# Down products two columns behind, up's last sum kept in PSUM, and the last additions shared: a feed-forward stage at the end of a two-layer kernel

## The chip, the core and the metric

The kernel runs on one core of a Trainium2 chip. The core has a matrix engine (TensorE, PE in the profile), a vector engine (VectorE, DVE), a scalar engine (ScalarE, ACT), a general engine (GpSimd, POOL) and a queue that issues transfers (SyncE, SP). PE multiplies a loaded 128x128 weight block with up to 512 columns and writes into PSUM, a small memory of eight banks; one bank holds 512 numbers for each of 128 partitions. DVE and ACT read and write PSUM and SBUF, the large on-chip memory; POOL works here on SBUF alone. The metric is the device time of one execution in microseconds (us). Three runs of the kernel before took 881.0, 881.89 and 882.64 us, median 881.89.

## What is computed

Two layers, each an attention and a feed-forward part with residual sums, over 8 sequences of 128 tokens of width 512. The change touches only the last part, a gated feed-forward network with integer weights and a scale for each group of 128 inputs:

```python
def dequantize(imatrix, scales, zeros, group_size, out_dtype):
    rs = jnp.repeat(scales, group_size, axis=0)
    rz = jnp.repeat(zeros, group_size, axis=0)
    return ((imatrix.astype(rs.dtype) - rz.astype(rs.dtype)) * rs).astype(out_dtype)

gate = jax.nn.silu(jnp.dot(x, gate_proj))     # (1024, 512) x (512, 1792)
up = jnp.dot(x, up_proj)
return jnp.dot(gate * up, down_proj)          # (1024, 1792) x (1792, 512)
```

Its input is the layer norm of x, and its result is added to x.

## The kernel before

Everything ahead of this part (about 714 of 881 us) is the same in both kernels. The feed-forward part works transposed: the hidden dimension of 1792 is cut into 14 columns of 128 (`NI = 14`), and the tokens into two halves of 512 (`hf`). The layer-normed input stands as a high and a low part (`xn2`), the weights as exact small integers, so a product of 512 tokens takes two matmuls, one for the low and one for the high part (L858, L859).

A *unit* (`unit`, L852) is one group of 128 inputs for one column and both halves: four matmuls into a PSUM tile of two banks (`f`; `ps_f` has four of them, which is all of PSUM), and then the scaling by the group's scale while the tile is emptied. The first unit of a sum is copied out by ACT (L863). A later one is added to the sum in SBUF either by DVE in one instruction (`scalar_tensor_tensor`, L869) or, for `eng == "A"`, by ACT, which copies it scaled into a tile `tmp` (L866, two buffers), and POOL, which adds `tmp` to the sum (L867).

For a column c there are four units for gate and four for up. Their sums are built in pairs: units 0 and 1 into one tile, 2 and 3 into another (L881: `a = g - g % 2`), and POOL adds the two tiles (`merge`, L892 to L894; letters `gm` and `um`). In the last column the four go into one tile, with no merge. Then ACT takes the silu (`S`, L900), DVE multiplies with up (`gated`, `H`, L904), ACT rounds the product to its high part `h_h` (`cast`, `C`, L911), and POOL subtracts to get the low part `h_l` (`rest`, `L`, L918; DVE does it for the last column). Four down units multiply h with the down weights and add into `acc`, 128 x 4 x 2 x 512 numbers in SBUF.

`ORDER` gives the order of the columns. Columns 0, 1 and 2 have had their first token half done earlier, among the last rounds of attention; what is left of them is half a column (units of two matmuls). They stand at the second, the fourth and the last place of `ORDER`. In the last four columns of the loop, `a0` to `a3` add the first-half down units of the last column.

The loop over the first 13 columns (L964 to L968) emits each column by a string of letters, in which `d` is a down unit of the column that `DOWN` names, `LAG = 3` columns earlier:

```python
emit(f"g0 d0 g2 g1 u0 g3 gm d1 u2 {a}u1 d3 d2 u3 um S" + (" H C L" if i < NI - 2 else ""), i)
```

A scheduler lays out the loop's instructions on their engines; each engine then works through its own list in order and waits where an input or a buffer isn't there. In PE's list every column of the loop reads, in units, g d g g u g d u u d d u from the column on that has down units. The tail (from L970) is laid out in the order in which it is written: the last column's gate and up units, between them the 12 down units of the three columns before it (`downs`, with a letter for the engine, V for DVE and A for ACT with POOL), its product, cast and rest, its four half down units, and the end: PE turns `acc` back in 32 transposes (L1009), DVE adds it to x in eight additions of 128x512 (L1011), and SP sends each one out (L1012).

Apart from the value of `LAG` (L118) the diff starts at L838; the functions that it touches and the loop are printed here.

Of the kernel before, what the change touches and what calls it, by code (L numbers as in the profile page):

```python
# [9 lines left out]
F32 = mybir.dt.float32  # L10
# [3 lines left out]
ALU = mybir.AluOpType  # L14
# [3 lines left out]
P = 128  # L18
D = 512
KT = D // P  # L20
NB = 8
HB = 4
TOK = HB * P
# [6 lines left out]
NI = IC // P  # L30
# [4 lines left out]
def f32(ap):  # L35
    return ap.bitcast(F32)
# [3 lines left out]
def tile_layers(ctx: ExitStack, tc: tile.TileContext, t, out: bass.AP):  # L40
    nc = tc.nc

    def pool(stack, name, bufs, space=None, side="left"):
        kw = {"side": side}
        if space is not None:
            kw["space"] = space
        return stack.enter_context(tc.tile_pool(name=name, bufs=bufs, reuse_waits="tile", **kw))
# [7 lines left out]
    ident = const.tile([P, P], F32, name="ident")  # L55
# [58 lines left out]
    xs = [const.tile([P, HB, D], F32, name=f"xs{hf}") for hf in range(2)]  # L114


    NE = 3
    LAG = 3  # L118
    skv = ctx.enter_context(ExitStack())
    cpool = pool(skv, "cpool", 1, side="right")  # L120
    kvp = pool(skv, "kvp", 2, side="right")
# [195 lines left out]
    A, B = layer0(0), layer0(1)  # L317
# [363 lines left out]
    for i in range(3 * NI):  # L681
        m, c = ("gate", "up", "down")[i % 3], i // 3
# [36 lines left out]
    xn2, xnb, xst = {}, {}, {}  # L719
# [118 lines left out]

    fw = pool(ctx, "fw", 3)
    fa = pool(ctx, "fa", 1)  # L840
    fh = pool(ctx, "fh", LAG)
    fp = pool(ctx, "fp", 2, side="right")
    ps_f = pool(ctx, "ps_f", 4, PSUM)

    acc = fa.tile([P, KT, 2, TOK], F32, name="acc")

    def weights(m, c):
        wf = fw.tile([P, D], F32R, name=f"wf_{m}")
        nc.sync.dma_start(f32(wf), wint[m, c])
        return wf  # L850

    def unit(eng, wf, g, rhs, s, dst, first, hs=(0, 1)):  # L852

        ps = ps_f.tile([P, 2, TOK], F32, name="f")
        w = wf[:, g * P : (g + 1) * P]
        for hf in hs:
            rh, rl = rhs(hf)
            nc.tensor.matmul(ps[:, hf, :], w, rl, start=True, stop=False)  # L858
            nc.tensor.matmul(ps[:, hf, :], w, rh, start=False, stop=True)  # L859
        sl = slice(hs[0], hs[-1] + 1)  # L860
        ps, dst = ps[:, sl, :], dst[:, sl, :]
        if first:
            nc.scalar.activation(dst, ps, AF.Copy, scale=s)  # L863
        elif eng == "A":
            a2 = fa.tile([P, 2, TOK], F32, name="tmp", bufs=2)[:, sl, :]
            nc.scalar.activation(a2, ps, AF.Copy, scale=s)  # L866
            nc.gpsimd.tensor_tensor(dst, dst, a2, ALU.add)  # L867
        else:
            nc.vector.scalar_tensor_tensor(dst, ps, s, dst, ALU.mult, ALU.add)  # L869

    def late(c):
        return nc.vector if c == ORDER[-1] else nc.gpsimd

    hts, wfs, gu, ths = {}, {}, {}, {}

    def up_unit(m, g, c):
        s_sb = sg_sb if m == "gate" else su_sb
        if g == 0:
            wfs[m] = weights(m, c)

        a = 0 if c == ORDER[-1] else g - g % 2  # L881
        if g == a:
            gu[m, g] = fp.tile([P, 2, TOK], F32, name=f"{m}{g}", bufs=2)
        unit(
            "V", wfs[m], g, lambda hf: (xn2[hf][0][:, g, :], xn2[hf][1][:, g, :]),
            s_sb[:, c, g : g + 1], gu[m, a], g == a, (1,) if c < NE else (0, 1),
        )

    def part(ap, c):
        return ap[:, 1:, :] if c < NE else ap  # L890

    def merge(m, c):  # L892
        a, b = (part(gu[m, g], c) for g in (0, 2))
        late(c).tensor_tensor(a, a, b, ALU.add)  # L894

    def silu(c):
        ga = part(gu["gate", 0], c)
        ths[c] = fh.tile([P, 2, TOK], F32, name="th", bufs=3)
        th = part(ths[c], c)
        nc.scalar.activation(th, ga, AF.Silu)  # L900

    def gated(c):
        th = hts[c] = ths.pop(c)
        nc.vector.tensor_tensor(part(th, c), part(th, c), part(gu["up", 0], c), ALU.mult)  # L904

    def cast(c):
        th = hts[c]
        hh, hl = (fh.tile([P, 2, TOK], F32R, name=f"h_{p}") for p in "hl")
        if c < NE and c != ORDER[-1]:
            nc.scalar.copy(hh[:, 0, :], early[c])  # L910
        nc.scalar.copy(part(hh, c), part(th, c))  # L911
        hts[c] = (th, hh, hl)

    def rest(c):
        th, hh, hl = hts[c]
        if c < NE and c != ORDER[-1]:
            late(c).tensor_tensor(hl[:, 0, :], early[c], f32(hh[:, 0, :]), ALU.subtract)
        late(c).tensor_tensor(part(hl, c), part(th, c), part(f32(hh), c), ALU.subtract)  # L918
# [5 lines left out]
    def down_unit(o, c, hs=None, eng=None):  # L924
        if o == 0 and hs != (1,):
            wfs["down", c] = weights("down", c)
        hh, hl = first_h if hs == (0,) else hts[c][1:]
        if eng is None:
            eng = "A" if o in on_act(c) else "V"
        unit(  # L930
            eng, wfs["down", c], o, lambda hf: (hh[:, hf, :], hl[:, hf, :]),
            sd_sb[:, o, c : c + 1], acc[:, o], c == ORDER[0], hs or (0, 1),
        )
# [4 lines left out]
    def first_half():  # L938
        c = ORDER[-1]
        first_h.extend(fh.tile([P, 1, TOK], F32R, name=f"h1_{p}", bufs=1) for p in "hl")  # L940
        nc.scalar.copy(first_h[0][:, 0, :], early[c])
        nc.gpsimd.tensor_tensor(first_h[1][:, 0, :], early[c], f32(first_h[0][:, 0, :]), ALU.subtract)


    ORDER = [c for i in range(NE - 1) for c in (NE + i, i + 1)] + list(range(2 * NE - 1, NI)) + [0]

    DOWN = {i: (i - LAG,) for i in range(LAG, NI + LAG)}

    def emit(seq, i):
        c = ORDER[i] if i < NI else NI  # L950
        for it in seq.split():
            k, j = it[0], it[1:]
            if k in "gu" and c < NI:
                m = "gate" if k == "g" else "up"
                merge(m, c) if j == "m" else up_unit(m, int(j), c)
            elif k == "a":
                down_unit(int(j), ORDER[-1], (0,))
            elif k == "d":
                for p in DOWN.get(i, ()):
                    down_unit(int(j), ORDER[p])  # L960
            elif k in "SHCL" and c < NI:
                {"S": silu, "H": gated, "C": cast, "L": rest}[k](c)

    for i in range(NI - 1):  # L964
        if i == NI - 6:
            first_half()
        a = f"a{i - NI + 5} " if i >= NI - 5 else ""
        emit(f"g0 d0 g2 g1 u0 g3 gm d1 u2 {a}u1 d3 d2 u3 um S" + (" H C L" if i < NI - 2 else ""), i)  # L968
    ET = mybir.EngineType
    with tc.manual_schedule(engines={ET.PE, ET.DVE, ET.Activation, ET.Pool}):  # L970

        c = ORDER[-1]
        p = iter([(o, ORDER[i]) for i in range(NI - 1 - LAG, NI - 1) for o in range(KT)])

        def downs(engs):
            for e in engs:
                down_unit(*next(p), eng=e)

        up_unit("gate", 0, c)
        up_unit("gate", 1, c)  # L980
        downs("A")
        up_unit("gate", 2, c)
        up_unit("gate", 3, c)
        gated(ORDER[-2])
        downs("A")
        up_unit("up", 0, c)
        silu(c)
        cast(ORDER[-2])
        rest(ORDER[-2])
        up_unit("up", 1, c)  # L990
        downs("V")
        up_unit("up", 2, c)
        up_unit("up", 3, c)
        downs("V")
        gated(c)
        cast(c)
        downs("AV")
        rest(c)
        downs("VAVVAV")
        for o, e in zip(range(KT), "VAVV"):  # L1000
            down_unit(o, c, (1,), e)
        for hf in range(2):
            xt = xs[hf]
            for b in range(0, HB, 2):
                tp = ps_f.tile([P, 2, TOK], F32, name="f")
                for i in range(2):
                    cols = slice((b + i) * P, (b + i + 1) * P)
                    for o in range(KT):
                        nc.tensor.transpose(tp[:, i, o * P : (o + 1) * P], acc[:, o, hf, cols], ident)  # L1009
                for i in range(2):  # L1010
                    nc.vector.tensor_tensor(xt[:, b + i, :], tp[:, i, :], xt[:, b + i, :], ALU.add)  # L1011
                    nc.sync.dma_start(out[hf * HB + b + i], xt[:, b + i, :])  # L1012


# [49 lines left out]
```

## Time and profile before

| | |
|---|---|
| runs | 881.0, 881.89, 882.64 us |
| profiled execution | 882.38 us |
| its span, first to last instruction | 880.6 us |
| feed-forward part, first to last instruction | 713.9 to 880.6 us |
| first matmul of the last column's gate | 845.21 us |
| end of the last addition to x | 876.43 us |

The page of the profile gives, for the whole span, the busy time of each engine and the chain of work that ended last. The timeline lists instructions in order of time: start, duration, engine, line, operation, output and inputs with their shapes, and in brackets how long the engine stood idle before it and what ended that. The waits sum up who waited for whom. The busy time by stretches gives for each piece of time the busy us of PE, PEld, DVE, ACT and POOL with the numbers of instructions, the clock that PE was granted (1.00 is full), the share of the DMA engines and GB/s. An engine that is behind its inputs shows no idle time; one that waits shows whom it waited for, and the last of several inputs is the one named.

### The profile page before, as it was taken

The numbers are of one execution on the slowest core, as the hardware profiler recorded it, in microseconds if no ns is written. First come the engines' busy times: TensorE is split into PE (matmuls) and PEld (weight loads), VectorE is DVE, ScalarE is ACT, GpSimd is POOL, SyncE is SP. The second block draws the span as 40 slices with busy tenths as digits, with TensorE's granted clock in tenths as the row PEclk, the third lists the DMA queues.
The fourth block names the chain that finished last, engine by engine and source line by source line (L and its number), as shares of the span: only waits on it lengthen the run. The fifth ranks groups of instructions, "written<-read, shape, count | busy, mean of one in ns | idle before, by whom it ended". The sixth has DMA issues, their size and how long they took to land.

```text
span 880.6 us, 14074 instructions
## 1 busy us (share of the span) xinstructions
PE 852.4 (97%) x4568; PEld 716.8 (81%) x4568; DVE 627.1 (71%) x1049; ACT 438.7 (50%) x1565; POOL 518.2 (59%) x571
## 2 busy tenths in 40 slices
PE   6999999999999999999999999999999989999985
PEld 5889998899788888888888888888878767788764
DVE  6513697775777777777777777666786887889887
ACT  5323444244544455544555444444555568666652
POOL 4551684234665555555555555765454568899884
PEclk9899999999999999999999999999999999999998
DMA  8522342524777778777777786544234412222102
GB/s 298 137 96 97 133 137 91 144 97 168 251 246 236 212 249 250 241 210 248 241 231 221 252 250 217 178 145 143 94 129 138 132 36 73 72 73 72 48 25 96
DMA packets 115833, 141.01 MB, mean 160 GB/s; under 512 B 14128, under 2 KB 59952, under 8 KB 115760
## 3 DMA queue, kind: packets, MB, share of 16 engines
q1 hardware_dynamic: 115760, 140.12, 50.6%
q8 instruction: 36, 0.59, 0.3%
q14 instruction: 37, 0.30, 0.1%
HBM read 97.62 MB, written 42.47 MB: 159 GB/s over the span
## 4 chain that ended last, share of the span: by engine, by line
PE 83%; POOL 6%; DVE 6%; ACT 2%; issue 2%; DMA 1%; SPq 0%; DVEq 0%; POOLq 0%; ACTq 0%
PE mm L74 9%; PE mm L76 9%; PE mm L75 9%; PE f L858 6%; PE o L76 6%; PE o L74 6%; PE o L75 6%; PE f L859 6%; PE s L540 6%; PE tr L567 3%; PE kv L76 3%; PE kv L75 3%; PE kv L74 3%; PE o L581 2%; PE o L579 2%
## 5 line engine op out<-in xcount | busy, mean ns | idle before, releaser
L562 POOL TENSOR_TENSOR pr<-pr,rs 128x512 f32<-128x512 f32 x64 | 66.6, 1040 | 176.5 <-DVE rs L560 173.6
L601 DVE TENSOR_TENSOR xs<-o,xs 128x512 f32<-128x512 f32 x64 | 44.2, 691 | 95.4 <-PE o L76 95.4
L74 PE MATMUL mm<-wq_l,xnT_h 128*128 128x512 f32 x256 | 105.4, 412 | 0.0
L76 PE MATMUL o<-wo_h,aT_l 128*128 128x512 f32 x256 | 100.0, 390 | 0.7 <-DVE aT_l L589 0.7
L74 PE MATMUL o<-wo_l,aT_h 128*128 128x512 f32 x256 | 100.1, 391 | 0.2 <-DVE wo_l L66 0.2
L76 PE MATMUL mm<-wq_h,xnT_l 128*128 128x512 f32 x256 | 100.2, 392 | 0.0
L75 PE MATMUL mm<-wq_h,xnT_h 128*128 128x512 f32 x256 | 100.0, 391 | 0.0
L75 PE MATMUL o<-wo_h,aT_h 128*128 128x512 f32 x256 | 99.7, 389 | 0.0
L571 ACT CAST pT_h<-tr 128x512 fp32r<-128x512 f32 x64 | 37.5, 585 | 121.2 <-PE tr L567 121.2
L554 ACT ACTIVATE pr<-s,nm 128x128 f32<-128x128 f32 x256 | 90.8, 373 | 3.3 <-DVE nm L548 3.0
L588 ACT CAST aT_h<-o 128x512 fp32r<-128x512 f32 x64 | 37.6, 587 | 103.8 <-PE o L581 103.8
L74 PE MATMUL kv<-wkv_l,cT_h 128*128 128x256 f32 x256 | 73.6, 288 | 0.0
L507 ACT ACTIVATE junkq<-mm 128x128 f32<-128x128 f32 x256 | 67.3, 279 | 12.5 <-PE mm L76 6.1
L76 PE MATMUL kv<-wkv_h,cT_l 128*128 128x256 f32 x256 | 73.3, 286 | 0.0
L75 PE MATMUL kv<-wkv_h,cT_h 128*128 128x256 f32 x256 | 72.9, 285 | 0.0
L348 POOL TENSOR_TENSOR rrq<-msq,nhalf 128x4 f32<-128x4 f32 x64 | 64.7, 1011 | 5.3
L540 PE MATMUL s<-kT,qT 128*128 128x128 f32 x512 | 67.6, 275 | 0.0
L540 PEld LDWEIGHTS s<-kT,qT 128*128 128x128 f32 x512 | 62.3, 192 | 0.1
L572 DVE TENSOR_TENSOR pT_l<-tr,pT_h 128x512 fp32r<-128x512 f32 x64 | 44.0, 688 | 22.7 <-ACT pT_h L571 22.7
L76 PEld LDWEIGHTS o<-wo_h,aT_l 128*128 128x128 f32 x256 | 48.1, 188 | 11.5 <-DVE aT_l L589 1.5
L76 PEld LDWEIGHTS mm<-wq_h,xnT_l 128*128 128x128 f32 x256 | 48.1, 188 | 10.7
L74 PEld LDWEIGHTS o<-wo_l,aT_h 128*128 128x128 f32 x256 | 48.1, 188 | 10.7 <-DVE wo_l L66 0.6
(234 smaller groups left out, 2448.8 us busy)
## 6 DMA issues: line engine op xcount, KB each, us to landing
q_d<-qb SPq DMA_DIRECT2D x64, 256.0 KB, 2.0
qT<-q_d SPq DMA_DIRECT2D x64, 256.0 KB, 4.1
wst<-in_qpT SPq DMA_DIRECT2D x36, 256.0 KB, 4.6
wst<-in_opT SPq DMA_DIRECT2D x36, 256.0 KB, 3.8
wkv<-in_kvT SPq DMA_DIRECT2D x8, 512.0 KB, 4.5
v_d<-vh SPq DMA_DIRECT2D x16, 256.0 KB, 2.0
v_d<-vl SPq DMA_DIRECT2D x16, 256.0 KB, 2.3
kT_d<-kT SPq DMA_DIRECT2D x16, 256.0 KB, 2.7
```

The lines of the kernel that those rows point to most:

```text
L74: nc.tensor.matmul(o, ah, bl, start=start, stop=False)
L75: nc.tensor.matmul(o, ah, bh, start=False, stop=False)
L76: nc.tensor.matmul(o, al, bh, start=False, stop=stop)
L348: nc.gpsimd.tensor_tensor(r[:, :n], ms[:, :n], nhalf[:, :n], ALU.pow)
L507: nc.scalar.activation(junk, qps[u][:, r * HD : (r + 1) * HD], AF.Square, accum_out=ssq[:, r : r + 1])
L540: nc.tensor.matmul(sp[:, r, :], qTs[u][:, r, :], kTt[blocks[j]][:, :, i, :], start=True, stop=True)
L554: nc.scalar.activation(pr[:, r, :], sps[u][:, r, :], AF.Exp, bias=nms[u][:, r : r + 1], accum_out=sm[:, r : r + 1])
L562: nc.gpsimd.tensor_tensor(pr, pr, rs.unsqueeze(2).to_broadcast([P, NQ, P]), ALU.mult)
L572: nc.vector.tensor_tensor(pl, tps[u], f32(ph), ALU.subtract)
L601: nc.vector.tensor_tensor(x, pos[u], x, ALU.add)
L858: nc.tensor.matmul(ps[:, hf, :], w, rl, start=True, stop=False)
L859: nc.tensor.matmul(ps[:, hf, :], w, rh, start=False, stop=True)
```

## The change

`LAG` goes from 3 to 2, so each column's down units stand two columns behind its gate and up units, and the tail has eight full down units in place of 12. The pool of h tiles keeps its three buffers. For the column before the last, up's four units are summed in one tile without a merge, and in this and the last column the fourth sum is written into its own PSUM tile (`eng == "P"`), from which the product reads it. The tail is written in a new order with other engine letters; `tmp` has four buffers. At the end three of the eight additions to x go to ACT (a copy out of PSUM) and POOL (the addition).

```diff
-    LAG = 3
+    LAG = 2
...
-    fh = pool(ctx, "fh", LAG)
+    fh = pool(ctx, "fh", 3)
...
+        elif eng == "P":
+            nc.vector.scalar_tensor_tensor(ps, ps, s, dst, ALU.mult, ALU.add)
+            return ps
         elif eng == "A":
-            a2 = fa.tile([P, 2, TOK], F32, name="tmp", bufs=2)[:, sl, :]
+            a2 = fa.tile([P, 2, TOK], F32, name="tmp", bufs=4)[:, sl, :]
...
-        a = 0 if c == ORDER[-1] else g - g % 2
+        one = c == ORDER[-1] or (m, c) == ("up", ORDER[-2])
+        a = 0 if one else g - g % 2
...
-        unit(
-            "V", wfs[m], g, lambda hf: (xn2[hf][0][:, g, :], xn2[hf][1][:, g, :]),
+        upf[c] = unit(
+            "P" if one and (m, g) == ("up", KT - 1) else "V", wfs[m], g, lambda hf: (xn2[hf][0][:, g, :], xn2[hf][1][:, g, :]),
...
-        nc.vector.tensor_tensor(part(th, c), part(th, c), part(gu["up", 0], c), ALU.mult)
+        up = upf.pop(c)
+        nc.vector.tensor_tensor(part(th, c), part(th, c), part(gu["up", 0], c) if up is None else up, ALU.mult)
...
-        emit(f"g0 d0 g2 g1 u0 g3 gm d1 u2 {a}u1 d3 d2 u3 um S" + (" H C L" if i < NI - 2 else ""), i)
+        if i < NI - 2:
+            emit(f"g0 d0 g2 g1 u0 g3 gm d1 u2 {a}u1 d3 d2 u3 um S H C L", i)
+        else:
+            emit(f"g0 d0 g2 g1 u0 g3 gm d1 u1 {a}u2 d3 d2 u3 S", i)
...
+        gated(ORDER[-2])
         up_unit("gate", 0, c)
         up_unit("gate", 1, c)
+        cast(ORDER[-2])
         downs("A")
+        rest(ORDER[-2])
         up_unit("gate", 2, c)
         up_unit("gate", 3, c)
-        gated(ORDER[-2])
-        downs("A")
+        downs("V")
         up_unit("up", 0, c)
         silu(c)
-        cast(ORDER[-2])
-        rest(ORDER[-2])
         up_unit("up", 1, c)
-        downs("V")
+        downs("VA")
         up_unit("up", 2, c)
         up_unit("up", 3, c)
+        gated(c)
+        downs("A")
+        cast(c)
         downs("V")
-        gated(c)
-        cast(c)
+        rest(c)
         downs("AV")
-        rest(c)
-        downs("VAVVAV")
+
+        def turn(hf, b, engs):
+            xt = xs[hf]
+            tp = ps_f.tile([P, 2, TOK], F32, name="f")
+            for i in range(2):
+                cols = slice((b + i) * P, (b + i + 1) * P)
+                for o in range(KT):
+                    nc.tensor.transpose(tp[:, i, o * P : (o + 1) * P], acc[:, o, hf, cols], ident)
+            for i, e in enumerate(engs):
+                x = xt[:, b + i, :]
+                if e == "A":
+                    a2 = fa.tile([P, 2, TOK], F32, name="tmp", bufs=4)[:, 0, :]
+                    nc.scalar.copy(a2, tp[:, i, :])
+                    nc.gpsimd.tensor_tensor(x, a2, x, ALU.add)
+                else:
+                    nc.vector.tensor_tensor(x, tp[:, i, :], x, ALU.add)
+                nc.sync.dma_start(out[hf * HB + b + i], x)
+
         for o, e in zip(range(KT), "VAVV"):
             down_unit(o, c, (1,), e)
-        for hf in range(2):
...
+        turn(0, 0, "VA")
+        turn(0, 2, "VA")
+        turn(1, 0, "AV")
+        turn(1, 2, "VV")
```

## The prediction

> **What bounds the kernel now.** I read the page first, then the chain of waits, then the timeline of the last 167 us (714 to 881), which is all that the diff touches: up to there the order on every engine is the same in both kernels. The page says that TensorE (PE) is the bound as a whole, and the chain of waits agrees:
>
> ```profile
> PE 852.4 (97%) x4568; PEld 716.8 (81%) x4568; DVE 627.1 (71%) x1049; ACT 438.7 (50%) x1565; POOL 518.2 (59%) x571
> ...
> PE 83%; POOL 6%; DVE 6%; ACT 2%; issue 2%; DMA 1%; SPq 0%; DVEq 0%; POOLq 0%; ACTq 0%
> ```
>
> The busy time by stretches (PE, PEld, DVE, ACT, POOL, granted clock, DMA share, GB/s) splits the part that matters in three:
>
> ```profile
> 713.93:750.00 36.07, 34.04 (x143) 26.12 (x144) 27.93 (x26) 29.58 (x35) 27.94 (x16) 1.00 0.25 73
> 750.00:845.20 95.20, 94.46 (x411) 76.38 (x410) 83.91 (x71) 62.33 (x59) 82.81 (x34) 1.00 0.20 59
> 845.20:880.60 35.40, 23.44 (x105) 17.45 (x103) 27.64 (x29) 10.24 (x12) 23.26 (x11) 0.90 0.22 75
> ```
>
> A start, a middle in which PE does not rest, and a tail in which it rests a third of the time. Matmuls of 512 columns start 0.2275 us apart (784.00, 784.22, 784.45 in the timeline), so a full unit (4 matmuls) costs PE 0.91, half a unit 0.455, and a full column of 12 units 10.9. The tail has the two long waits, both for POOL or for what POOL holds up:
>
> ```profile
> 849.76 3.37 DVE L904 TENSOR_TENSOR th<-th,up 128x1024 f32<-128x1024 f32 x1 [0.42 <-POOL up L894]
> ...
> 853.25 0.50 PE L858 MATMUL f<-xnT_l,wf_up 128*128 128x512 f32 x1 [2.44 <-ACT tmp L866]
> ...
> 861.95 0.48 PE L858 MATMUL f<-h_l,wf_down 128*128 128x512 f32 x1 [2.19 <-issue]
> ```
>
> The product in L904 takes 1.22 us elsewhere (at 793.62), here 3.37. The wait before 853.25 is for a copy into tmp (L866), which itself waited 3.57 for POOL to give back one of the two tmp buffers. The one before 861.95 ends with a DVE sum (860.57 to 861.84) that stood behind the last product (858.37, 2.27 for 512 columns), which ended only when POOL's h_l did (860.10).
>
> **The change, part by part.** The profiled execution took 882.38 us with a span of 880.6; the median of the three runs is 881.89. I sum against 882.38 and move the result down by 0.5. The waits of the changed kernel come from working its built order forward from 713.9: an instruction starts when its engine is free and its inputs are there, with the durations of the rows (PE 0.2275 and 0.1 at each restart; POOL 2.41 or 1.29; DVE 1.28 or 0.75, products 1.22 or 0.68; ACT 1.12 or 0.69, casts 1.05 or 0.62). The same working over the order of before puts its last addition at 875.98, where the trace has 876.43.
>
> *LAG 2, at the start.* In the built order PE's queue in each column is g d g g u g d u u d d u. In before the third column (from 726.24) had no d; now its second unit is the first down product of column one, and PE is in order, so everything waits for that column's h_l:
>
> ```profile
> 726.24 0.50 PE L858 MATMUL f<-xnT_l,wf_gate 128*128 128x512 f32 x1 [0.64 <-ACT up L863]
> ...
> 727.71 2.21 POOL L894 TENSOR_TENSOR up<-up,up 128x512 f32<-128x512 f32 x1 [0.83 <-DVE up L869]
> ...
> 728.55 0.62 ACT L900 ACTIVATE th<-gate 128x512 f32<-128x512 f32 x1
> ...
> 730.07 1.04 ACT L911 CAST h_h<-th 128x1024 fp32r<-128x1024 f32 x1
> ...
> 731.18 2.41 POOL L918 TENSOR_TENSOR h_l<-th,h_h 128x1024 fp32r<-128x1024 f32 x1 [1.27 <-ACT h_h L911]
> ...
> 734.37 0.47 PE L858 MATMUL f<-h_l,wf_down 128*128 128x512 f32 x1
> ```
>
> In the new ScalarE order one copy (L863) that stood between the silu at 728.55 and the cast is gone, so the cast runs 729.1 to 730.1; POOL is free at 729.9 and writes h_l 730.2 to 732.6. PE has done its gate unit at 727.27 and stands until 732.7: 5.4 us, in which before did 24 matmuls. Behind the waiting matmul stand all the other units of the column, so ScalarE and DVE run dry and nobody catches up meanwhile. The idle that before has between 733 and 750 (0.26 ahead of 734.37, 1.44 ahead of 749.41, restarts: 2.0) shrinks to about 1.1. Cost +4.5; bounds +3.4 (all 2.0 regained) and +5.4 (none). SP issues each down weight a column earlier, past one up weight; a 256 KB issue lands in 2 to 5 us and these are issued some 10 us ahead, so I price it at 0; without that lead, a few us once.
>
> *The clock after that wait.* In before a stretch with PE busy 1.18 of 3.36 is followed by one at half clock:
>
> ```profile
> 859.60:862.96 3.36, 1.18 (x6) 0.86 (x6) 3.36 (x4) 2.22 (x3) 1.01 (x2) 1.00 0.00 0
> 862.96:866.36 3.40, 3.40 (x10) 2.62 (x9) 2.17 (x3) 0.41 (x1) 3.40 (x2) 0.50 0.01 2
> ```
>
> A wait of 5.4 should bring 3.4 us at half clock, 1.7 lost if it all falls on work, 0 if none does. I take 1.2, as part of it can fall into the wait itself. The Trainium skill (TensorE: Matmul & The Clock Gate, Part 1) wants a wholly idle window of about 3.4 us for this; the row shows that a window busy for a third is enough. By the page a wait of 5.4 holds a whole window in 0.6 of the phases, an estimate of 1.0 for this term; the sum would be 0.2 lower.
>
> *LAG 2, in the middle.* A chain closes on itself: first down product of a column, four more units, DVE's sum of the last gate unit, POOL's gate merge (held up by L904), POOL's h_l. In before:
>
> ```profile
> 776.74 0.39 PE L858 MATMUL f<-h_l,wf_down 128*128 128x512 f32 x1
> ...
> 781.54 1.29 DVE L869 SCALAR_TENSOR_TENSOR gate<-f,sg_sb,gate 128x1024 f32<-128x1024 f32 x1 [0.53 <-PE f L859]
> ...
> 782.91 3.33 POOL L894 TENSOR_TENSOR gate<-gate,gate 128x1024 f32<-128x1024 f32 x1 [0.45 <-DVE gate L869]
> ...
> 786.20 2.41 POOL L918 TENSOR_TENSOR h_l<-th,h_h 128x1024 fp32r<-128x1024 f32 x1
> ```
>
> From 776.74 to 788.61 it is 11.87 against a column of 10.9. With three columns of lag nobody needs that h_l for another column; with two, the next column's first d needs it at once: 1.0 late, each time that POOL takes the merge ahead of h_l. In the built order it does so in four columns running (the first eats slack) and once more near the end. Working it forward: three waits of 0.9, two of 0.45, two of 0.27, restarts 0.7: 4.8, against 1.95 of idle in before between 750 and 845. Cost +2.8; bounds 0 (slack covers it) and +8 (1.0 in each of nine columns).
>
> *Work moved.* One column's four down units leave the tail for the loop: +3.64 there, -3.64 in the tail.
>
> *The tail.* From the last column's first gate unit (845.21) to the last addition (876.43) before takes 31.2: units 16.4, waits 8.7 (2.6 at 853.25, 2.4 at 861.95, 1.6 of half clock, 0.5 twice, restarts), 6.1 from the last down product on. After: units 12.7. In the last full column one up copy (ScalarE, 1.12) becomes a DVE sum (1.28), and the merge on POOL (2.41) is gone; the last sum writes PSUM. The nearest row that writes PSUM (L546, 0.69 for 512) costs what the one into SBUF does (L601, 0.69), so I take 1.28. The product then reads one operand from PSUM, one from SBUF, as L869 does, and of its 98 sums none took over 1.29 however busy POOL was; so 1.28, with 3.37 as the other end. With four tmp buffers the copy no longer waits for POOL, and the wait at 853.25 goes; with the last product at 0.75 the one at 861.95 loses its cause. The larger h and tmp pools cost no instruction: 0. What is late next: POOL writes the last full column's h_l only after three additions to acc (1.6 of PE wait), then DVE's own h_l (two SBUF operands) behind one more (1.7); with small ones and restarts 5.2. The end grows to 7.0: ScalarE copies 0.59 and POOL adds 1.29 where DVE took 0.61, and POOL's three adds end last. Together 24.9: -6.3. Bounds: units alone, -3.6, if every wait comes back; -14.5 if no wait is left and the end takes 4.
>
> The Trainium skill (SBUF — State Buffer, Who interferes with whom) says that a DVE instruction with one SBUF input does not contend with POOL. By it the product costs what the sums do; by the row of 849.76, unrelieved, the tail would save about 2 less.
>
> Sum: 3.64 + 4.5 + 1.2 + 2.8 - 6.3 = +5.8; 888.2 for a profiled execution, **887.7** for the median.
>
> **The rivals.**
> - *The middle keeps up* (for: POOL is busy 82.8 of 95.2 there, so it can catch up; against: the 11.87 above is a latency, not a load). 887.7 - 2.8 = 884.9.
> - *The middle falls behind in every column* (for: the chain is the same in all; against: where h_l stands ahead of the merge it is 2 us shorter). +8 in place of +2.8: 892.9.
> - *Faster*: the tail loses every wait, since its new order puts each down unit where an operand is ready; 24.9 becomes 12.7 + 4 = 16.7, and the time 879.5. For: 14.8 of the 31.2 are waits and ending. Against: the last column's chain (silu, product, cast, h_l, then four half units) is still serial. It decides from 7.6 us saved beyond the 6.3.
> - *No change*: the start costs its lower bound (3.4), the clock nothing and the middle 1.0: +3.64 + 3.4 + 1.0 - 6.3 = +1.7, 883.6. For: each is within its bounds. Against: all three must hold.
>
> **How the numbers follow.** 0.2% (1.8 us, 880.1 to 883.7) is about what can be told from no change. Likeliest 0.70, with 885.9 to 889.7 as its own range (start -1.1 or +0.9, clock 0 to 1.7, 0.5 of working); the middle keeps up 0.14; falls behind 0.08; no change 0.05; faster 0.03. The range for 8 in 10 leaves out the falling behind, the no change and the faster case and takes in most of the second: 884.6 to 890.8. Faster 0.03, same 0.05, slower 0.92.
>
> **What would show it.** PE's first matmul from h_l near 732.7 with some 5 us idle before it, released by POOL; a stretch at 0.5 clock from about 730 or 733; waits of about 0.9 for POOL's h_l ahead of the first d in three columns near 786 to 812; from the last column's first gate to the last addition about 25; the last product at 1.28 or less. I am wrong if the first d comes before 730, or if the middle has no such waits, or if the tail takes under 18 us.

## The result, and the profile after

The changed kernel takes 889.47 us (median of four runs, 888.75 to 889.82) against 881.44 for the kernel before (four runs, 880.67 to 882.64): 1.0089 times as long, 95% interval 1.0071 to 1.0106. The forecast was 887.7, in a range of 884.6 to 890.8. The profiled execution took 889.66 us with a span of 887.9, 7.3 more than before.

The page's engine totals and chain. PE works as long as before; in the chain PE's share has fallen from 83% to 68% and POOL's has grown from 6% to 14%. Eight points are 71 us, far more than the 7.3 that were lost: the shares say through whom the chain runs, not what it costs.

```profile
PE 853.3 (96%) x4568; PEld 716.7 (81%) x4568; DVE 621.7 (70%) x1047; ACT 441.1 (50%) x1567; POOL 520.0 (59%) x573
...
PE 68%; POOL 14%; issue 8%; DVE 6%; ACT 2%; DMA 1%; SPq 0%; POOLq 0%; DVEq 0%; ACTq 0%
```

What PE waited for in the feed-forward part, by releaser (us in total, times, longest). In before POOL's h_l does not appear there at all:

```profile
PE f L858 <- POOL h_l L923: 10.4, 8, 5.4
PE f L858 <- DVE h_l L923: 1.6, 1, 1.6
```

The busy time by stretches (PE, PEld, DVE, ACT, POOL, clock, DMA share, GB/s): the start, the middle, and from the last column's first gate unit on:

```profile
712.87:750.00 37.13, 30.96 (x119) 23.74 (x120) 20.75 (x21) 24.16 (x28) 21.66 (x12) 0.91 0.19 54
750.00:858.44 108.44, 104.65 (x451) 83.47 (x450) 92.27 (x80) 68.62 (x67) 92.25 (x39) 1.00 0.21 60
858.44:887.90 29.46, 17.95 (x89) 13.36 (x87) 20.55 (x23) 11.12 (x14) 21.81 (x12) 0.93 0.22 81
```

At the start PE is idle for 6.2 of 37.1 us, where before had 2.0 of 36.1, and its clock has fallen from 1.00 to 0.91. The timeline there shows both:

```profile
726.67 2.18 POOL L898 TENSOR_TENSOR up<-up,up 128x512 f32<-128x512 f32 x1 [0.85 <-DVE up L872]
...
729.13 2.63 POOL L923 TENSOR_TENSOR h_l<-th,h_h 128x1024 fp32r<-128x1024 f32 x1 [0.29 <-ACT h_h L916]
...
731.82 0.79 PE L858 MATMUL f<-h_l,wf_down 128*128 128x512 f32 x1 [5.42 <-POOL h_l L923]
732.41 0.63 PE L859 MATMUL f<-h_h,wf_down 128*128 128x512 f32 x1
732.84 0.63 PE L858 MATMUL f<-h_l,wf_down 128*128 128x512 f32 x1
```

The first product from h_l stands 5.6 us behind the gate unit, for POOL; then products start 0.43 us apart, not 0.23. The stretches of 3.4 us over that place show how the clock went:

```profile
727.00:730.41 3.41, 0.00 (x0) 0.00 (x0) 1.41 (x2) 3.19 (x5) 3.12 (x2) 1.00 0.00 0
730.41:733.83 3.42, 2.01 (x5) 1.62 (x6) 0.00 (x0) 0.00 (x0) 3.42 (x3) 0.51 0.00 0
733.83:737.24 3.41, 3.41 (x10) 2.64 (x9) 0.00 (x0) 2.23 (x2) 0.41 (x1) 0.50 0.03 5
737.24:740.65 3.41, 3.41 (x17) 2.79 (x16) 2.57 (x2) 1.62 (x2) 0.00 (x0) 0.99 0.04 8
```

One stretch without a product, then two at half clock, the first of them busy for 2.01 of 3.42, the second all the time; then full clock. The products of 731.82 to 737.42 take 2.64 us more than at 0.2275 each.

In the middle, POOL's list beside the first product of a column:

```profile
781.87 3.33 POOL L898 TENSOR_TENSOR gate<-gate,gate 128x1024 f32<-128x1024 f32 x1 [0.96 <-DVE gate L872]
785.15 2.40 POOL L923 TENSOR_TENSOR h_l<-th,h_h 128x1024 fp32r<-128x1024 f32 x1
...
793.91 3.32 POOL L898 TENSOR_TENSOR gate<-gate,gate 128x1024 f32<-128x1024 f32 x1 [1.64 <-DVE gate L872]
...
787.61 0.50 PE L858 MATMUL f<-h_l,wf_down 128*128 128x512 f32 x1 [0.87 <-POOL h_l L923]
799.63 0.50 PE L858 MATMUL f<-h_l,wf_down 128*128 128x512 f32 x1 [0.85 <-POOL h_l L923]
```

(The last two lines are PE's, from the same stretch.) The gate merge goes ahead of h_l, and a column lasts 12.02 us (787.61 to 799.63) where its units are 10.9. There are three such waits of 1.0 (787.61, 799.63, 811.67), and smaller ones at 753.82, 823.71 and 847.50. In the tail:

```profile
860.89 1.22 DVE L909 TENSOR_TENSOR th<-th,f 128x1024 f32<-128x1024 f32 x1
...
869.10 0.50 PE L858 MATMUL f<-h_l,wf_down 128*128 128x512 f32 x1 [1.36 <-POOL h_l L923]
869.15 0.69 DVE L909 TENSOR_TENSOR th<-th,f 128x512 f32<-128x512 f32 x1
...
872.45 2.13 DVE L923 TENSOR_TENSOR h_l<-th,h_h 128x512 fp32r<-128x512 f32 x1
874.63 0.50 PE L858 MATMUL f<-h_l,wf_down 128*128 128x512 f32 x1 [1.59 <-DVE h_l L923]
...
879.62 3.71 POOL L1021 TENSOR_TENSOR xs<-tmp,xs 128x512 f32<-128x512 f32 x3 [1.55 <-ACT tmp L1020]
```

The products out of PSUM take 1.22 and 0.69, where before had 3.37 and 2.27; two long waits for h_l are left (1.5 and 1.8 us), and POOL's additions end last.

### The profile page after: what moved, and what is told of

The parts are those of the page before. It is cut to its first block, busy times and chain, and to the rows that moved or that the text cites. A ratio compares the mean times of both kernels' runs of the same rounds, so it can differ in the third digit from the quotient of the medians.

```text
span 887.9 us, 14066 instructions
## 1 busy us (share of the span) xinstructions
PE 853.3 (96%) x4568; PEld 716.7 (81%) x4568; DVE 621.7 (70%) x1047; ACT 441.1 (50%) x1567; POOL 520.0 (59%) x573
## 4 chain that ended last, share of the span: by engine, by line
PE 68%; POOL 14%; issue 8%; DVE 6%; ACT 2%; DMA 1%; SPq 0%; POOLq 0%; DVEq 0%; ACTq 0%
PE mm L74 8%; PE mm L76 8%; PE mm L75 8%; PE o L76 6%; PE o L75 6%; PE o L74 6%; PE s L540 6%; PE tr L567 3%; POOL acc L870 3%; PE f L858 2%; PE f L859 2%; POOL gate L898 2%; POOL h_l L923 2%; POOL up L898 2%; PE kv L76 2%
## 5 line engine op out<-in xcount | busy, mean ns | idle before, releaser
L858 PE MATMUL f<-h_l,wf_down 128*128 128x512 f32 x112 | 45.6, 408 | 12.4 <-POOL h_l L923 10.4
L76 PEld LDWEIGHTS o<-wo_h,aT_l 128*128 128x128 f32 x256 | 48.1, 188 | 11.5 <-DVE aT_l L589 1.5
```

Source lines behind the costliest of these rows:

```text
L76: nc.tensor.matmul(o, al, bh, start=False, stop=stop)
```

## How the experiments are read

The times of one kernel lie 1 to 4 us apart (before, on one chip, 878.93 to 883.0 in 18 runs), and most of that lies ahead of the part in question: the first product of the feed-forward part comes anywhere between 711.1 and 714.2 in these profiles, though everything ahead of it is the same in all kernels. So each profile is also cut at three places: the first matmul with a gate weight, the first one of the last column's gate, and the end of the last addition to x. Between the first two lies the *loop*, between the last two the *tail*. For the kernel after these are 712.87, 858.44 and 883.33 (879.62 and 3.71): 145.57 and 24.89. The other kernels are cut alike. Where two kernels have the same work in them, the loops agree within 0.4 us (after, 6, 7 and 9; before, 3, 10 and 11) and the tails within 0.03 (after, 1, 2 and 9). In 5 and 8 a wait of the tail has moved ahead of the cut (0.77 at 862.17 in after, 0.96 at 856.31 in 5), so these two are judged by loop and tail together.

| kernel | median us | ratio to before (95%) | loop | tail | both |
|---|---|---|---|---|---|
| before | 881.44 | | 131.28 | 31.22 | 162.50 |
| after | 889.47 | 1.0089 (1.0071 to 1.0106) | 145.57 | 24.89 | 170.46 |
| 1: downs late in the third column | 882.66 | 1.0016 (1.0004 to 1.0029) | 138.05 | 24.89 | 162.94 |
| 2: products in the wait | 886.38 | 1.0059 (1.0036 to 1.0082) | 142.37 | 24.92 | 167.29 |
| 3: LAG 3, the rest of the change | 877.55 | 0.9967 (0.9952 to 0.9983) | 131.27 | 27.68 | 158.95 |
| 4: LAG 2 alone | 893.65 | 1.0139 (1.0116 to 1.0162) | 145.92 | 29.36 | 175.28 |
| 5: gate in one tile in the middle | 886.95 | 1.0067 (1.0052 to 1.0082) | 143.44 | 24.27 | 167.71 |
| 6: last sum of up in SBUF | 892.40 | 1.0127 (1.0112 to 1.0142) | 145.59 | 27.07 | 172.66 |
| 7: last additions on DVE | 888.99 | 1.0090 (1.0074 to 1.0105) | 145.75 | 24.59 | 170.34 |
| 8: 1 and 5 together | 879.52 | 0.9983 (0.9973 to 0.9992) | 135.90 | 24.30 | 160.20 |
| 9: two tmp buffers | 889.46 | 1.0105 (1.0086 to 1.0124) | 145.37 | 24.91 | 170.28 |
| 10: as 3, other engine letters | 876.46 | 0.9951 (0.9936 to 0.9966) | 131.34 | 25.70 | 157.04 |
| 11: before with four tmp buffers | 878.59 | 0.9985 (0.9976 to 0.9994) | 131.30 | 29.08 | 160.38 |

The ratios go against runs of the kernel before on the same chip, whose medians were 881.01 for 1 to 4, 881.05 for 5 to 8, 880.81 for 9 and 10, and 880.16 for 11.

The theory was the prediction's: LAG 2 costs the moved work, one long wait at the start with a slow clock behind it, and a late h_l in the middle; the tail's new parts give back less than that. The rivals: the start's loss would be swallowed later; the slow clock costs nothing; the middle has nothing to do with the merge; the tail's gain is only the moved work.

## The start: experiments 1 and 2

**1. The down units behind the others in the third column.**

```diff
+        if i == LAG:
+            emit("g0 g2 g1 u0 g3 gm u2 u1 u3 um S H C L d0 d1 d2 d3", i)
-        if i < NI - 2:
+        elif i < NI - 2:
```

> The changed kernel (889.5 us), but the third column of the order, the first that has down units, carries its four down units behind its own eight units; every other column as in the change. Theory (the start's wait and the slow clock behind it are most of the loss): the wait of 5.6 us goes, and the 2.6 us of half clock with it, while about 1 us of the idle of the kernel before comes back: 882.5 us, 881.5 to 884, with no stretch at half clock between 726 and 745. Rival A (slack later in the loop would have swallowed the start's wait, and the loss comes from the middle and the tail): above 887. Rival B (the slow clock falls into time that is lost anyway): only the wait goes, 884.5 to 886.

Measured 882.66. The wait and the half clock are gone, and PE is busy throughout (busy time by stretches, columns as above):

```profile
725.20:731.82 6.62, 5.97 (x25) 4.65 (x26) 4.70 (x6) 5.86 (x8) 4.52 (x4) 1.00 0.30 79
731.82:737.00 5.18, 5.18 (x24) 4.08 (x23) 3.45 (x3) 4.47 (x6) 5.18 (x3) 1.00 0.40 104
```

The loop is 7.52 us shorter than in after. Of what went, a wait of 0.79 at 740.32 came back. The middle's waits stand as they were (1.03 at 781.38, 793.42 and 805.46, 0.43 and 0.44 later): slack later on swallows nothing of the start. Rival A falls with its 887; B's 884.5 lies above the median, and the clock's share is measured next.

**2. Products in the wait.**

```diff
         w = wf[:, g * P : (g + 1) * P]
+        if rep:
+            wg = wfs["gate"][:, :P]
+            for _ in range(rep):
+                nc.tensor.matmul(ps[:, 0, :], wg, xn2[0][0][:, 0, :], start=True, stop=True)
```

`rep` is 22 for the very first down unit and 0 elsewhere.

> The changed kernel, but ahead of the first down product of all, into the same PSUM tile, 22 products of a gate weight block are put that the product then overwrites, 5.0 us of work inside the 5.6 us in which PE stood. The result is the same. Theory (the idle window sends the clock to half, and that costs 2.6 us): no half clock behind 732, the first product from h_l at the same place, 2.6 us less: 886.9, 886.2 to 887.8. Rival (the half clock costs nothing, or the products delay what follows): 889 to 890.5.

Measured 886.38, loop 3.20 us shorter than in after:

```profile
727.49:732.49 5.00, 5.00 (x24) 4.13 (x22) 2.19 (x3) 3.72 (x5) 4.30 (x2) 1.00 0.10 35
732.49:737.70 5.21, 5.21 (x24) 4.32 (x23) 1.71 (x2) 3.24 (x3) 3.14 (x3) 1.00 0.00 0
...
735.21 0.39 PE L862 MATMUL f<-h_l,wf_down 128*128 128x512 f32 x1
```

One thing did not go as meant: the scheduler moved the first product from h_l behind three other units, to 735.21. PE still pays 5.0 us for the extra products, where it stood for 5.6 before: 0.6 of the 3.2 is this, and the other 2.6 is what thirteen slow products lost in after (2.64 above). The half clock has its own price, and idle time is its cause.

In the six profiles that keep the wait (after, 4, 5, 6, 7 and 9) the slow products cost 2.3 to 2.9 us, added up in the same way, and end 4.8 to 6.1 us behind the wait.

## The middle: experiments 5 and 8

**5. No gate merge in the sixth to the eleventh column.**

```diff
-        one = c == ORDER[-1] or (m, c) == ("up", ORDER[-2])
+        one = c == ORDER[-1] or (m, c) == ("up", ORDER[-2]) or (m == "gate" and 5 <= ORDER.index(c) < 11)
...
     def merge(m, c):
+        if m == "gate" and (5 <= ORDER.index(c) < 11):
+            return
```

> The changed kernel, but in the sixth to the eleventh column of the order gate's four units are summed in one tile, as in the last column: POOL has no gate merge there, and of each column one copy on ScalarE becomes a sum on DVE. The start and the tail are as in the change. Theory (the five waits for POOL's h_l between 787 and 848, 3.9 us, come from the gate merge that stands ahead of h_l): they go, a few tenths come back as waits for DVE: 3.2 us less, 886.3, 885.3 to 887.3. Rival A (PE is held up by DVE just as much, since DVE takes 1.28 us more in each of these columns): 889 to 891. Rival B (the waits are carried over from the start, and have nothing to do with the merge): the waits stay, 889 to 890.

Measured 886.95; loop and tail together are 2.75 us shorter. POOL now starts h_l as soon as its input is cast:

```profile
783.06 2.42 POOL L925 TENSOR_TENSOR h_l<-th,h_h 128x1024 fp32r<-128x1024 f32 x1 [3.37 <-ACT h_h L918]
...
794.20 2.42 POOL L925 TENSOR_TENSOR h_l<-th,h_h 128x1024 fp32r<-128x1024 f32 x1 [3.35 <-ACT h_h L918]
...
816.59 0.50 PE L858 MATMUL f<-xnT_l,wf_up 128*128 128x512 f32 x1 [0.39 <-DVE gate L872]
828.50 0.50 PE L858 MATMUL f<-xnT_l,wf_up 128*128 128x512 f32 x1 [0.22 <-DVE acc L872]
856.31 0.50 PE L858 MATMUL f<-xnT_l,wf_gate 128*128 128x512 f32 x1 [0.79 <-ACT tmp L869]
```

The five waits of 787 to 848 (1.03, 1.01, 1.02, 0.42, 0.43: 3.9 us) are gone, and 0.55, 0.38 and part of 0.96 have come in their place, for DVE and ScalarE. POOL idles 3.4 us ahead of each of these h_l now. That it was the order of the two instructions and not the amount of POOL's work that held PE up is argued from this idle time; h_l ahead of the merge was not run. The start's wait is still there (5.6 at 731.82), and in experiment 1 the middle's waits stand without it, so they don't hang on it, and rival B falls.

**8. Both.** The edits of 1 and 5 together.

> The down units behind the eight of the third column, and gate summed in one tile in the sixth to the eleventh: the start's wait, the slow clock and the middle's waits are all taken away at LAG 2. Theory (these and the moved work are all that LAG 2 costs, and they add up): 882.5 less 3.2, 879.3, 878 to 880.5, faster than the kernel before by the tail's net gain. Rival (with the start's wait gone the engines stand closer, and the middle's cost returns elsewhere): 881 to 883.

Measured 879.52, 0.9983 of before (0.9973 to 0.9992). Experiment 1 saved 7.52 of loop and tail, 5 saved 2.75, both together 10.26: the two costs add up, to 0.01. What LAG 2 then still costs against the same tail with LAG 3 (experiment 3 below, 158.95) is 160.20 - 158.95 = 1.25 us, and the tail's parts, worth 3.5 there, pay for it. What summing gate in one tile would do at LAG 3 was not run.

## LAG against the rest: experiments 3, 4 and 10

**3. All but LAG.**

```diff
-    LAG = 2
+    LAG = 3
...
         rest(c)
-        downs("AV")
+        downs("AVVAVV")
```

> All of the change but LAG: the columns stand three apart as before, so the tail has twelve full down units (the letters of the last call are AVVAVV in place of AV); up's last sums in PSUM, four tmp buffers, the new order and the shared additions stay. Theory (the loss is LAG's, the tail's parts gain 2.7 us beside the moved work of 3.6): the loop as before, the tail 28.4 us against 31.2: 879.0, 877.5 to 880.5, faster than the kernel before. Rival (the tail's gain is only the moved work, and its parts give nothing by themselves): 881 to 883.

Measured 877.55: faster than the kernel before. The loop is before's to 0.01, and the tail, with the same twelve full down units as before, 27.68 against 31.22. In its timeline:

```profile
846.71 1.22 DVE L909 TENSOR_TENSOR th<-th,f 128x1024 f32<-128x1024 f32 x1
854.97 0.69 DVE L909 TENSOR_TENSOR th<-th,f 128x512 f32<-128x512 f32 x1
...
863.01 0.50 PE L858 MATMUL f<-h_l,wf_down 128*128 128x512 f32 x1 [0.84 <-ACT tmp L869]
```

Neither wait for h_l is left, as four more down units stand ahead of each; the longest is this one, of 1.0, for a copy. The tail's parts are worth 3.5 us, and the rival (only the moved work) falls. LAG 2 in place of 3, with these parts, costs 170.46 - 158.95 = 11.5 us.

**4. LAG 2 alone**, in the kernel before:

```diff
-    LAG = 3
+    LAG = 2
...
-        downs("VAVVAV")
+        downs("AV")
```

> The kernel before with LAG 2 alone (the h pool keeps three buffers, the last call of down units has AV in place of VAVVAV); tail order, tmp buffers, sums and last additions as before. Theory: the loop as in the changed kernel (+14.4 us), the tail 3.6 us shorter by the moved work and up to 3 us of new waits, since the last full column's h_l still comes late in it and fewer units stand ahead of it: 894, 892 to 896. Rival (the other parts of the change cost more than they give): 889 or less.

Measured 893.65. The loop is nearly after's (145.92), and the tail is only 1.86 us shorter than before's, though 3.64 of work has left it:

```profile
861.54 3.37 DVE L904 TENSOR_TENSOR th<-th,up 128x1024 f32<-128x1024 f32 x1 [0.41 <-POOL up L894]
...
865.03 0.50 PE L858 MATMUL f<-xnT_l,wf_up 128*128 128x512 f32 x1 [2.43 <-ACT tmp L866]
...
871.84 0.50 PE L858 MATMUL f<-h_l,wf_down 128*128 128x512 f32 x1 [3.35 <-POOL h_l L918]
```

In the old order the last full column's h_l comes late, and with a column less of down units ahead of it PE waits 3.75 for it. So the other parts, which a rival blamed, save 4.5 us of the tail at LAG 2 (29.36 to 24.89).

**10. A version that beats both.** Experiment 3 with the early additions on DVE:

```diff
-        downs("AVVAVV")
+        downs("VVAVVA")
...
-        turn(1, 0, "AV")
+        turn(1, 0, "VV")
```

> LAG 3 with the tail's parts, as in the experiment of 877.6 us, but the last call of down units in the tail has the letters VVAVVA in place of AVVAVV, and DVE makes six of the last eight additions, with ScalarE and POOL two. Theory (in that experiment two waits of 0.6 and 1.0 us are left ahead of the last column's half down units, for POOL's chain of five additions to acc, and POOL's three last additions end 0.7 us after DVE's; both shrink when the early additions go to DVE): 876.0, 875 to 877.5, 0.6% faster than the kernel before. Rival (DVE is then late instead, with its own chain of sums): 877.5 to 879.

Measured 876.46, 0.9951 of before (0.9936 to 0.9966). The tail is 1.98 us shorter than in 3. Of this, 0.88 lies ahead of the last down product (it starts 18.98 us into the tail, at 861.43, against 19.86, at 864.13), where the wait of 1.0 in the half down units is 0.45. The other 1.10 lies behind it (6.72 to the end of the last addition against 7.82), although the transposes wait 1.2 for POOL's last addition to acc, after three of them, where in 3 all of them wait 0.6 for a sum of DVE's:

```profile
861.66 0.49 PE L1015 MATMUL f<-ident,acc 128*128 128x128 f32 x3
...
863.11 3.39 PE L1015 MATMUL f<-ident,acc 128*128 128x128 f32 x29 [0.96 <-POOL acc L870]
```

The two edits weren't tried apart. The intervals of 3 and 10 overlap; that 10 is the better rests on the cuts.

## The tail's parts: experiments 6, 7, 9 and 11

**6. Up's last sum in SBUF.**

```diff
-            "P" if one and (m, g) == ("up", KT - 1) else "V", wfs[m], g, lambda hf: ...
+            "V", wfs[m], g, lambda hf: ...
```

> The changed kernel, but up's last sum goes to its SBUF tile in the last two columns too, and both products read two SBUF operands. Theory (such a product is held up while POOL works, as the one of 3.37 us in the kernel before; from PSUM it takes 1.22): the two products take up to 2 us longer each, the tail 2.8 us longer in all: 892.3, 891 to 893.5. Rival (the products beside POOL's work cost the same with two SBUF operands, and the tail's gain is from its order and the tmp buffers): 889 to 890.3.

Measured 892.40, the tail 2.18 us longer:

```profile
861.26 3.25 DVE L909 TENSOR_TENSOR th<-th,up 128x1024 f32<-128x1024 f32 x1
...
865.23 0.50 PE L858 MATMUL f<-h_l,wf_down 128*128 128x512 f32 x1 [2.83 <-DVE gate L872]
...
871.54 2.80 DVE L909 TENSOR_TENSOR th<-th,up 128x512 f32<-128x512 f32 x1
```

The products take 3.25 and 2.80 with both operands in SBUF, beside POOL's additions, and 1.22 and 0.69 with one in PSUM. The wait ahead of 865.23 (3.0, in after 0.8 at 862.17) is for the gate sum that stands behind the first of them.

**7. The last additions on DVE alone.**

```diff
-        turn(0, 0, "VA")
-        turn(0, 2, "VA")
-        turn(1, 0, "AV")
+        turn(0, 0, "VV")
+        turn(0, 2, "VV")
+        turn(1, 0, "VV")
```

> The changed kernel, but DVE makes all eight of the last additions, as in the kernel before. Theory (ScalarE's copy and POOL's addition, 0.59 and 1.24, take as long as DVE saves): the end is the same or 0.9 us shorter: 888.9, 888.4 to 889.7. Rival (the shared additions save time, as eight additions of 0.61 on one engine are longer than five): 890 to 891.

Measured 888.99, ratio 1.0090 as in after: no difference that the times can tell. The tail is 0.30 shorter, where equal tails agree within 0.03: sharing three additions gains nothing here, and by the cut loses 0.3. The rival falls.

**9. Two tmp buffers.**

```diff
-            a2 = fa.tile([P, 2, TOK], F32, name="tmp", bufs=4)[:, sl, :]
+            a2 = fa.tile([P, 2, TOK], F32, name="tmp", bufs=2)[:, sl, :]
...
-                    a2 = fa.tile([P, 2, TOK], F32, name="tmp", bufs=4)[:, 0, :]
+                    a2 = fa.tile([P, 2, TOK], F32, name="tmp", bufs=2)[:, 0, :]
```

> The changed kernel with two tmp buffers in place of four. Theory as the prediction had it (the wait of 2.6 us ahead of 853.25 in the kernel before goes because the copies have four buffers): with two it comes back, 891 to 892. Rival (in the new order POOL has given tmp back before the next copy comes, and the copies never need more than two): 889.5, 888.6 to 890.2.

Measured 889.46, tail 24.91: no difference. The prediction's reason falls. In the new order the copies don't need the two extra buffers.

**11. Four tmp buffers in the kernel before.**

```diff
-            a2 = fa.tile([P, 2, TOK], F32, name="tmp", bufs=2)[:, sl, :]
+            a2 = fa.tile([P, 2, TOK], F32, name="tmp", bufs=4)[:, sl, :]
```

> The kernel before with four tmp buffers in place of two, and nothing else. Theory (in the old order the wait of 2.6 us ahead of 853.25 is for tmp alone, as the prediction read it, and half a us or so of it comes back later): 881.1 less 2, 879.0, 878.3 to 879.8. Rival A (the wait is POOL's, which holds up what follows just as long): 880.5 to 881.5, no change. Rival B (all of it goes and more behind it, the wait ahead of 861.95 and the slow clock too): below 877.5.

Measured 878.59, 0.9985 of before (0.9976 to 0.9994); the tail 29.08, 2.14 shorter. So in the old order the buffers do matter. Of the two long waits of before, one has moved, and the other is 0.5:

```profile
847.40 3.39 DVE L904 TENSOR_TENSOR th<-th,up 128x1024 f32<-128x1024 f32 x1 [0.40 <-POOL up L894]
...
851.50 0.50 PE L858 MATMUL f<-h_l,wf_down 128*128 128x512 f32 x1 [2.14 <-DVE up L869]
858.25 0.50 PE L858 MATMUL f<-h_l,wf_down 128*128 128x512 f32 x1 [0.33 <-POOL h_l L918]
```

ScalarE's copy no longer waits, and at once PE waits as long for DVE, which is held up by the slow product of 847.40. The buffer was one of two causes that stood side by side. The half clock is still there too, now behind this wait (0.60 and 0.65 from 851.50 to 856.00). What is won is the other wait: 0.5 where before has 2.4 ahead of 861.95. There the last product had started behind POOL's h_l; now it starts just ahead of it:

```profile
857.69 2.41 POOL L918 TENSOR_TENSOR h_l<-th,h_h 128x1024 fp32r<-128x1024 f32 x1
...
858.37 2.27 DVE L904 TENSOR_TENSOR th<-th,up 128x512 f32<-128x512 f32 x1
```

```profile
855.26 0.68 DVE L904 TENSOR_TENSOR th<-th,up 128x512 f32<-128x512 f32 x1
...
855.32 2.88 POOL L918 TENSOR_TENSOR h_l<-th,h_h 128x1024 fp32r<-128x1024 f32 x1
```

The first pair is of before, the second of this run: the same product took 2.27 us there and 0.68 here. So most of the gain of 2.14 seems to hang on a lead of 0.06 us, which no run has tried apart.

## Why the prediction was right, and where a size was off

The feed-forward part took 7.96 us more (loop +14.29, tail -6.33) against +5.8 in the sum; it began 1.06 earlier in this execution, and 0.40 more lies behind the last addition, which makes the span's 7.3. The sum was 2.2 short: 1.4 in the clock, the rest in the middle (0.45) and the start (0.3). The order of events was as forecast: the first product from h_l at 731.8 behind a wait for POOL, half clock from 730.4 on, three waits of 1.0 from 787.6 to 811.7, a tail of 24.9.

- *Work moved, +3.64.* Experiments 3 and 4 hold the units apart; right by construction.
- *The start, +4.5.* The wait was 5.6 (5.4 forecast), for POOL's h_l of column one, which took 2.63 and not 2.41; PE's first product from it came at 731.8 in an execution that began 1.06 earlier. Ahead of 754 PE idles 5.59 + 0.25 + 0.67 in after and 0.26 + 1.44 in before: +4.8. Confirmed by 1.
- *The clock, +1.2.* **This is the step that was mis-sized.** It was put at 1.2, with 1.7 as its bound, and cost 2.64. The prediction took one half-clock stretch of 3.4 us from the row of 862.96 and let part of it fall into the wait. There the work began at 861.95, 1.0 ahead of the stretch, so the stretch was busy from end to end. Here it began in the middle of one: that stretch, busy for 2.01 of 3.42, was followed by another one at half clock. The Trainium skill (TensorE: Matmul & The Clock Gate, Part 1) has the other half of its rule ready for this: full speed comes back after a busy window of about 3.4 us, and windows run free of the work. The rows agree, if a window that is idle for 1.4 us does not count as busy. The prediction had weighed only the half of the rule that sends the clock down.
- *The middle, +2.8.* What is left of the loop's 14.29 is 14.29 - 3.64 - 4.8 - 2.6 = 3.25. The waits stood where they were forecast (1.0, 1.0, 1.0 and 0.4 in consecutive columns and 0.4 near the end), and 5 shows that they go with the gate merge.
- *The tail, -6.3.* Measured -6.33, and not by errors that cancel: units 12.74 (12.7 forecast), from the first transpose on 6.75 (7.0), waits and restarts the other 5.4 (5.2). The two waits named as next came with 1.5 and 1.8 us, forecast 1.6 and 1.7. The size of the PSUM product was right (1.28; it is 1.22), and 6 shows that it carries 2.2 us of the gain. The Trainium skill (SBUF — State Buffer, Who interferes with whom) says that a DVE instruction with two SBUF inputs contends with POOL's reads of SBUF and one with a single SBUF input does not. The rows agree: 1.22 with one SBUF operand, 3.25 with two, beside the same two additions of POOL.
- *One reason was wrong inside a right sum.* The prediction credited the end of the wait of 853.25 to four tmp buffers. By 9 the new order does without them. By 11 they only change, in the old order, whom PE waits for at that place (2.3 us for DVE, behind the slow product), and by 6 the slow product brings a wait of 3.0 into the new order. That points to the short product as what ended the wait; the short product in the old order was not run.

Of the rivals, *no change* needed the clock at nothing and the start at 3.4, and neither held; *the middle falls behind in every column* needed waits of 1.0 in nine columns, and there were three; *the middle keeps up* needed none; *faster* needed a tail of 16.7.

## What to carry to other kernels

Shortening the distance between producer and consumer takes work out of the tail, but leaves every column's chain through three engines less time before PE needs its result: before doing it, follow the chain from one column's first consumer to the next one's, and look which short instruction stands behind a long one on the engine that feeds it. Here PE, standing for 5.6 us, paid a second time in its clock, with another 2.6; putting the consumer behind work that was ready anyway (experiment 1) brought back one wait of 0.8 and saved 7.5 us on balance. And parts of a change should be priced alone: here the tail's parts with the old distance (877.6, and 876.5 with other engine letters) beat both kernels.

## What the runs showed of the hardware

- A stretch of 3.4 us at half clock in which PE was busy for 59% (2.01 of 3.42 us) was followed by another one, and so was one of experiment 4 that was busy for 76% (2.60 of 3.41, 729.22 to 732.63). At full clock, one that was busy for 63% (2.14 of 3.40, after, 723.60 to 727.00) was followed by full clock, one that was busy for 46% (1.55 of 3.40, experiment 4, 722.40 to 725.80) by half. With the work beginning inside such a stretch, the price of one long wait was 2.3 to 2.9 us in six profiles, not 1.7 at most.
- DVE's h_l of 128x512, two SBUF operands, took 0.68 us in before (861.77), 1.03 in experiment 3 (856.78), 1.67 in 6 (875.46) and 2.13 in after (872.45): the same instruction. POOL was idle beside the first. In the other three an addition of POOL's was under way when it started, and it ended 0.6 us after POOL had gone on to its next one (at 857.22, 876.53 and 873.97).
- Most of the scatter from execution to execution came from ahead of the part studied (its start moved by 3.1 us, while equal loops agreed within 0.4 and equal tails within 0.03).
